# A graph convolution and a graph attention in one kernel: transposes by 32x32 blocks on VectorE and plain transfers, in place of transposing transfers

## The chip, the cores and the metric

The kernel runs on one core of a Trainium2 chip. The metric is the device time of one execution in microseconds (us), from outside; the span of the profile lies within it. TensorE is called PE in the profile (PEld is its loading of stationary operands), VectorE is DVE, ScalarE is ACT, GpSimd is POOL; SP is the queue that issues all transfers.

## What is computed

16-bit arithmetic is not used: everything is float32. x has 128 graphs of 128 nodes and 512 features; adj is one 128x128 matrix for all of them.

```
h = relu(layernorm(x));  x = x + norm_adj @ (h @ W0) + b0         # layer 0
h = relu(layernorm(x))                                            # layer 1, 8 heads of 64
q, k, v = h @ Wq + bq, h @ Wk + bk, h @ Wv + bv
scores = q k^T / 8 + (1 - adj) * -1e9                             # per graph and head
x = x + (softmax(scores) @ v) @ Wo + bo
```

norm_adj is adj scaled by the inverse roots of its row sums on both sides.

## The kernel before, in words

**Groups and blocks.** The 128 graphs are worked in 32 groups of 4. In step t of the outer loop five blocks of matmuls follow one another: W (the projection by W0 for group t+1), Q and K (queries and keys of group t), V (values of group t), Y (the projection by Wo for group t-1). Each block is a product of 512x512 by 512x512, done as a Strassen product with seven products of 256x256, four of which are divided once more into seven (class `Projection`, lines 395 on). A block has seven steps, 0 to 6. The last phases of a block's seventh product are put off: `tail` (L393, filled and emptied in `step`, L523 on) runs them in steps 1 and 2 of the next block. At the beginning of step V0 stand the attention's own matmuls: `attend` (L901) for the group before and `scores` (L831).

**Halves.** Every matmul of 128 output rows is given as two of 64 (`halves`, L136 to L140), each into its own half of the array and of the output's partitions. A float32 matmul of the code is two passes in the trace, so it stands there as two records.

**Operands.** h and the attention's output are needed with the features on the partitions. Three tiles, `op_mix`, `op_norm` and `op_att`, hold such an operand: 40 slots of 128x128, of which 28 are the seven blocks of the outer product and 12 more the inner sums (`combine`, L376 on; `combine_one`, L86 to L94, runs on GpSimd as a rule). In V the operand h is stationary and the weights move; in Q and K the weights are stationary and h moves.

**The transposes before.** h of groups 2 to 30 is transposed by transfers: `split_h` (L753 on) copies on ScalarE the two 16-bit halves of each float32 word into two planes, `write_h` (L760) writes them to DRAM, and `turn_h` (L766) reads them back with a transposing transfer. The same is done for the softmax's output: `split_att` (L875, L876) and `turn_att` (L879), into the buffer of the graph before, so that five buffers `att_buf` go round for four graphs. The first groups and the last use TensorE: `transpose_h` (L742) with 16 transposes of 16-bit halves per graph, `transpose_att` (L886) with 8 transposes of float32.

**The order.** The scheduler doesn't choose it. `plan` is a table of places: `at(t, "Q2b", f, ...)` puts a function at the second gap of step 2 of block Q in turn t (letter of block, step, and gap: none is ahead of the step's matmuls, b after them, c after the step's other reads). Each engine executes its instructions in that order, so a place decides where in every queue a step's instructions stand. VectorE reads the matmuls' results from the eight PSUM banks (`add`, L448; `read`, L463), and a bank is filled again only after its reads. Weights are reloaded from DRAM in every turn in five parts (`reload_w`, L1088).

Of the kernel before, what the change touches and what calls it, by code (L numbers as in the profile page):

```python
# [85 lines left out]
def combine_one(engine, t, left, pair, step):  # L86


    def twice(n):
        x, y = (slot_of(left, k, n) for k in pair)  # L90
        return t[:, x : y + 1 : y - x, :]

    out, x, y, minus = step
    engine.tensor_tensor(twice(out), twice(x), twice(y), ALU.subtract if minus else ALU.add)  # L94
# [3 lines left out]
def kernel(  # L98
# [38 lines left out]
    def halves(out, lhsT, rhs, **flags):  # L137

        for y in range(0, P, P // 2):
            nc.tensor.matmul(out[y : y + P // 2], lhsT[:, y : y + P // 2], rhs, **flags)  # L140
# [16 lines left out]
    planes_dram = [dp.tile([P, 2, H * P], U16, tag=f"planes_{b}", name=f"planes_{b}") for b in range(GB)]  # L157
    h_dram = [dp.tile([P, 2, H * P], U16, tag=f"planes_h_{y}", name=f"planes_h_{y}") for y in range(2)]
# [25 lines left out]
    class Weight:  # L184
# [6 lines left out]
        def slot(self, k, n):  # L191
            return self.t[:, slot_of(False, k, n), :]

# [96 lines left out]
    def combine_inner(name, engine, steps=range(9)):  # L290
        for k in steps:
            pair, step = INNER[k]
            combine_one(engine, w_sb[name].t, False, pair, step)
# [68 lines left out]
    class Operands:  # L362
        def __init__(self, name):
            self.t = op.tile([P, SLOTS, P], F32, tag=name, name=name)

        def blocks(self, i):
            return self.t[:, LEFT_AT[i] : LEFT_AT[i] + 4, :].rearrange("p (c j) n -> p c j n", c=2)

        def slot(self, i, n):
            return self.t[:, slot_of(True, i, n), :]  # L370

        def blocks_of(self, b):
# [3 lines left out]
            return self.t[:, first + j : first + 8 : 2, :]  # L376

        def combine(self, engine, inner=True, then=None, within=None):
# [6 lines left out]
            if inner:  # L385
                for step in FIRST_LEFT:
                    combine_one(within, self.t, True, (S1, S4), step)
                for step in WINOGRAD_LEFT:
                    combine_one(within, self.t, True, (A12, A22), step)


    op_mix, op_norm, op_att = (Operands(f"op_{k}") for k in "aho")
    tail = []  # L393

    class Projection:
# [13 lines left out]
        def product(self, out, product, fresh):  # L409
# [3 lines left out]
            left, right = self.left.blocks(i), self.right.blocks(k)  # L413
            for c in range(2):
                for r in range(2):
                    start = fresh and c == 0 and r == 0
                    if self.stay:
                        self.matmul(out[:, r], left[:, c], right[:, c, r * P : (r + 1) * P], start)
                    else:
                        self.matmul(out[:, r], left[:, c, r, :], right[:, c, :], start)  # L420
# [237 lines left out]
    def gcn_mix(g, b):  # L658
# [7 lines left out]
        src = pa.rearrange("p (c n) -> p c n", c=NC)  # L666
        if g == 1 and b < 2:
            nc.vector.tensor_copy(op_a[g].blocks_of(b), src)
        else:
            nc.scalar.copy(op_a[g].blocks_of(b), src)  # L670
# [60 lines left out]
    def transpose_h(g, b):  # L731
# [5 lines left out]
        planes = pt.bitcast(BF16).rearrange("p (z c n) -> p z c n", z=2, c=NC)  # L737
        words = h2.bitcast(BF16).rearrange("n (c f z) -> n z c f", c=NC, z=2)
        for z in range(2):
            for c in range(NC):  # L740
                for y in range(0, P, P // 2):
                    nc.tensor.transpose(planes[y : y + P // 2, z, c, :], words[:, z, c, y : y + P // 2], ident16)  # L742
        nc.scalar.copy(
            op_h[g].blocks_of(b).bitcast(U16).rearrange("p c (n z) -> p c n z", z=2),
            pt.bitcast(U16).rearrange("p (z c n) -> p c n z", z=2, c=NC),
        )

    def h_planes(g, half):

        t = qs[g - 1][:, 2 * half : 2 * half + 2, :].bitcast(U16)  # L750
        return t.rearrange("n c f -> n (c f)")

    def split_h(g, b):  # L753
        half, j = divmod(b, 2)
        h2 = hs.pop((g, b)).bitcast(U16).rearrange("n (c f z) -> n z c f", c=NC, z=2)
        planes = h_planes(g, half).rearrange("n (z c j f) -> n z c j f", z=2, c=NC, j=2)
        nc.scalar.copy(planes[:, :, :, j, :], h2)

    def write_h(g, half):
        nc.sync.dma_start(h_dram[half], h_planes(g, half).rearrange("n (z f) -> n z f", z=2))  # L760

    def turn_h(g, half):
        op_h[g] = op_norm
        first = LEFT_AT[S1 if half else A11]
        blocks = op_norm.t.bitcast(U16)[:, first : first + 8, :]
        nc.sync.dma_start_transpose(out=blocks, in_=h_dram[half].rearrange("n z f -> (n z) f"))  # L766

    def attention_operands(g):
        op_h[g].combine(nc.vector if g < 2 else nc.gpsimd, g > 0, within=nc.gpsimd)
# [42 lines left out]
    def att_of(g, b):  # L812


        return att_buf[(b - g) % (GB + 1)]
# [46 lines left out]
    def softmax_end(g, b):  # L862
# [3 lines left out]
        if g == 1 or g == 0 and b >= 2:  # L866
            for h in range(H):
                nc.scalar.activation(att[:, h, :], att[:, h, :], AF.Identity, bias=0.0, scale=rsm[:, h : h + 1])
        else:
            nc.gpsimd.tensor_tensor(att, att, rsm.unsqueeze(2).to_broadcast([P, H, P]), ALU.mult)  # L870

    def split_att(g, b):
        halves = att_of(g, b).bitcast(U16).rearrange("q h (k z) -> q z (h k)", z=2)
        planes = att_of(g, b - 1).bitcast(U16).rearrange("q h k -> q (h k)").rearrange("q (z j) -> q z j", z=2)
        nc.scalar.copy(planes, halves)  # L875
        nc.sync.dma_start(planes_dram[b], planes)  # L876

    def turn_att(g, b):
        nc.sync.dma_start_transpose(out=att_of(g, b - 1).bitcast(U16), in_=planes_dram[b].rearrange("q z j -> (q z) j"))  # L879
# [10 lines left out]
    def attend(g, b):  # L890
        if g not in op_o:
            op_o[g] = op_norm if g == NG - 1 else op_att
        aT = att_of(g, b if turned_in_place(g, b) else b - 1)
# [4 lines left out]
        for c in range(NC):  # L898
            for p in range(2):
                h = 2 * c + p  # L900
# [361 lines left out]
```

## Time and profile before

| | |
|---|---|
| time, median of 3 runs | 2200.97 us (2200.22 to 2202.0) |
| the profiled execution | 2200.75 us, its span 2199.0 us |
| granted TensorE clock | 0.999 |
| busy ScalarE, of the span | 1393.8 us, 63% |
| transfers | 595.48 MB, 90.6% of the 16 engines' time in the main queue; 389073 of 530613 packets under 512 bytes |
| one group | 67.4 us (1013.1 to 1080.5) |
| ScalarE's splitting copies of attention (L875) | 121, 1894 ns each, 229.2 us |
| transposing transfers | 121 of attention, 58 of h; median 5.9 and 6.8 us from issue to landing |

How to read it: in a row of a group the last number before the bar is how often it stood there, behind the bar come the busy time as a union and the mean duration of one. Matmuls overlap, so their busy time is much shorter than count times mean; the spacing of their starts is what counts. In the timeline each row has the start in us from the span's start, the length of a run of equal instructions, the engine, the line, what is written and read, and how many. A form like 128*64 tells that a matmul uses 128 rows and 64 columns of the array. In the table of stretches the columns are the stretch, its length, and busy us with the number of instructions for PE, PEld, DVE, ACT and POOL, then the granted clock, the DMA share and GB/s.

### The profile page before, as it was taken

What the parts mean: (1) busy time and instruction counts of PE and PEld (TensorE: products, weight loads), DVE (VectorE), ACT (ScalarE), POOL (GpSimd) and SP (SyncE); (2) the same over time, 40 slices, a digit from 0 to 9 for tenths busy, and PEclk for the clock granted to TensorE, in tenths of its full rate; (3) what the DMA queues carried; (4) which work ended last, traced back from release to release, by engine and by line L of the source; (5) the groups of instructions that cost most, each with busy time, mean ns of one, the idle gap of its engine ahead of it and who ended that gap; (6) DMA issues with size and microseconds to landing.
All of it is one profiled execution on the core that took longest, in us unless ns stands there. A gap on an engine that the chain in (4) does not pass through costs nothing.

```text
span 2199.0 us, 77713 instructions
## 1 busy us (share of the span) xinstructions
PE 2186.2 (99%) x31749; PEld 1879.6 (85%) x31749; DVE 1774.9 (81%) x4244; ACT 1393.8 (63%) x3604; POOL 1886.1 (86%) x2049
## 2 busy tenths in 40 slices
PE   9999999999999999999999999999999999999999
PEld 7788888888888888888888888888888888888887
DVE  7777888878888778888788887788877888878876
ACT  4577665765666666666656676566666565765654
POOL 7988988898889898888988898888889888998754
PEclk9999999999999999999999999999999999999999
DMA  5489999999999999999999999999999999999982
GB/s 165 173 260 289 290 293 292 256 284 307 263 288 287 259 297 280 293 296 244 294 312 262 294 271 269 302 286 276 290 259 289 293 279 298 263 276 298 263 261 84
DMA packets 530613, 595.48 MB, mean 271 GB/s; under 512 B 389073, under 2 KB 396369, under 8 KB 529745
## 3 DMA queue, kind: packets, MB, share of 16 engines
q1 hardware_dynamic: 530256, 590.50, 90.6%
q8 instruction: 251, 4.11, 0.8%
q14 instruction: 106, 0.86, 0.1%
HBM read 358.68 MB, written 137.89 MB: 226 GB/s over the span
## 4 chain that ended last, share of the span: by engine, by line
PE 97%; DVE 1%; issue 0%; POOL 0%; DMA 0%; ACT 0%; SPq 0%; POOLq 0%; DVEq 0%; ACTq 0%
PE bank_a L140 37%; PE bank_d L140 22%; PE bank_b L140 11%; PE bank_c L140 11%; PE pa L140 5%; PE bank_d L831 3%; PE po L901 3%; PE pss L831 1%; PE bank_b L901 1%; PE bank_a L901 1%; PE bank_b L831 1%; PE paT L886 0%; DMA xt<-in_x_dram 0%; DVE xt L448 0%; POOL w L282 0%
## 5 line engine op out<-in xcount | busy, mean ns | idle before, releaser
L858 ACT ACTIVATE att<-att,nmx 128x128 f32<-128x128 f32 x1024 | 396.1, 393 | 0.5 <-DVE nmx L850 0.5
L140 PE MATMUL bank_a<-op_h,w 128*64 128x256 f32 x2976 | 353.5, 380 | 0.0
L870 POOL TENSOR_TENSOR att<-att,rsm 128x1024 f32<-128x1024 f32 x122 | 231.7, 1900 | 110.8 <-DVE rsm L865 98.3
L875 ACT COPY att<-att 128x2048 uint16<-128x2048 uint16 x121 | 229.2, 1894 | 114.6 <-POOL att L870 114.5
L448 DVE TENSOR_TENSOR xt<-xt,bank_d 128x512 f32<-128x512 f32 x610 | 270.3, 468 | 11.0 <-PE bank_d L140 0.5
L140 PEld LDWEIGHTS bank_a<-op_h,w 128*64 128x64 f32 x2976 | 207.9, 137 | 81.6 <-issue 0.5
L140 PE MATMUL bank_d<-op_h,w 128*64 128x128 f32 (+1 forms) x3424 | 221.7, 275 | 0.1
L94 POOL TENSOR_TENSOR op_o<-op_o 128x256 f32<-128x256 f32 x297 | 212.4, 739 | 10.1
L788 ACT ACTIVATE q<-bank_a,bqk 128x256 f32<-128x256 f32 x192 | 79.8, 466 | 211.5 <-PE bank_a L140 211.3
L94 POOL TENSOR_TENSOR op_a<-op_a 128x256 f32<-128x256 f32 x279 | 198.5, 734 | 9.6
L94 POOL TENSOR_TENSOR op_h<-op_h 128x256 f32<-128x256 f32 x270 | 191.2, 733 | 11.5 <-DVE op_h L384 2.1
L140 PEld LDWEIGHTS bank_d<-op_h,w 128*64 128x64 f32 x3424 | 195.0, 137 | 7.1 <-POOL w L282 0.5
L858 ACT ACTIVATION_READ_ACCUMULATOR att<-att,nmx 128x1 f32 x1024 | 196.6, 192 | 0.0
L140 PE MATMUL bank_a<-w,op_o 128*64 128x256 f32 x1536 | 182.2, 379 | 0.0
L140 PE MATMUL bank_a<-w,op_h 128*64 128x256 f32 x1488 | 178.0, 381 | 0.0
L140 PE MATMUL bank_a<-w,op_a 128*64 128x256 f32 x1488 | 176.5, 379 | 0.0
L463 DVE TENSOR_TENSOR xt<-bank_a,xt 128x512 f32<-128x512 f32 x252 | 166.8, 683 | 3.1 <-PE bank_a L140 3.1
L850 DVE TENSOR_REDUCE nmx<-att 128x8 f32<-128x1024 f32 x128 | 154.9, 1210 | 0.0
L356 POOL TENSOR_TENSOR xt<-xt,b_o 128x1024 f32<-128x1024 f32 x62 | 147.2, 2376 | 0.0
L140 PEld LDWEIGHTS bank_a<-w,op_o 128*64 128x64 f32 x1536 | 107.5, 137 | 41.2
L351 ACT ACTIVATE h<-op_o,nb,rs 128x512 f32<-128x512 f32 x112 | 91.8, 820 | 76.2 <-POOL nb L340 76.2
L140 PEld LDWEIGHTS bank_a<-w,op_h 128*64 128x64 f32 x1488 | 102.4, 137 | 43.7
(188 smaller groups left out, 5779.8 us busy)
## 6 DMA issues: line engine op xcount, KB each, us to landing
w<-wd_v SPq DMA_DIRECT2D x155, 512.0 KB, 4.9
w<-wd_o SPq DMA_DIRECT2D x155, 512.0 KB, 9.0
w<-wd_q SPq DMA_DIRECT2D x150, 512.0 KB, 8.3
w<-wd SPq DMA_DIRECT2D x145, 512.0 KB, 5.3
planes<-att SPq DMA_DIRECT2D x121, 512.0 KB, 6.3
out_dram<-xt SPq DMA_DIRECT2D x62, 512.0 KB, 7.4
planes_h<-q SPq DMA_DIRECT2D x58, 512.0 KB, 3.2
op_o<-in_x_dram SPq DMA_DIRECT2D x56, 512.0 KB, 9.8
```

The lines of the kernel that those rows point to most:

```text
L94: engine.tensor_tensor(twice(out), twice(x), twice(y), ALU.subtract if minus else ALU.add)
L140: nc.tensor.matmul(out[y : y + P // 2], lhsT[:, y : y + P // 2], rhs, **flags)
L351: nc.scalar.activation(h, src[:, j, :], AF.Relu, bias=nb[:, j : j + 1], scale=rs[:, j : j + 1])
L356: engine.tensor_tensor(t, src, bias.unsqueeze(1).to_broadcast([P, t.shape[1], D]), ALU.add)
L448: nc.vector.tensor_tensor(dst, dst, src, f)
L463: nc.vector.tensor_tensor(t, src.rearrange("p (r f) -> p r f", r=2), t, ALU.add)
L831: nc.tensor.matmul(pss[p][:, c, :], qs[g][rows, c, cols], ks[g][rows, c, cols], start=True, stop=True)
L850: nc.vector.tensor_reduce(nmx, att_of(g, b), AX.X, ALU.max, negate=True)
L858: nc.scalar.activation(att[:, h, :], att[:, h, :], AF.Exp, bias=nmx[:, h : h + 1], scale=1.0, accum_out=sm[:, h : h + 1])
L870: nc.gpsimd.tensor_tensor(att, att, rsm.unsqueeze(2).to_broadcast([P, H, P]), ALU.mult)
L875: nc.scalar.copy(planes, halves)
L901: nc.tensor.matmul(po[p * HD : (p + 1) * HD, c * P : (c + 1) * P], vs[g][:, b, h * HD : (h + 1) * HD], aT[:, p * NC + c, :], start=True, s ...
```

## The change

The transposing transfers, the planes and their 16-bit copies go. In their place VectorE transposes 32x32 blocks into one spare buffer (`att_buf[4]`), a plain transfer writes that to DRAM, and four plain transfers read it back, each into 32 partitions, in runs of 1 KB. What arrives is transposed but stands in four quarters: the 128 columns of a slot lie in four pieces of 32, one in each quarter of the tile. `op_norm` is read and written in quarters from here on, and a stationary operand in quarters is given to TensorE as four matmuls of 32 columns in place of two of 64. That holds for V of groups 0 to 30, and for the last group's Y, whose operand is `op_norm` too. A moving operand in quarters is read with two more steps. `transpose_h` now uses float32 transposes of 128x128 (4 per graph). Weight sums of k and v and steps of attention in the first groups get other places, as do layer norm and h of all groups. In the rows with three places the first is that of turn 1, the second that of the last turn, the third that of all others.

```diff
     def halves(out, lhsT, rhs, **flags):
-        for y in range(0, P, P // 2):
-            nc.tensor.matmul(out[y : y + P // 2], lhsT[:, y : y + P // 2], rhs, **flags)
...
+        if len(lhsT.shape) == 3:
+            parts = [lhsT[:, q] for q in range(lhsT.shape[1])]
+        else:
+            parts = [lhsT[:, y : y + P // 2] for y in range(0, P, P // 2)]
+        rows = P // len(parts)
+        for y, part in enumerate(parts):
+            nc.tensor.matmul(out[y * rows : (y + 1) * rows], part, rhs, **flags)
...
+    spare = att_buf[GB].rearrange("p h k -> p (h k)")
...
-    op_mix, op_norm, op_att = (Operands(f"op_{k}") for k in "aho")
+    op_mix, op_norm, op_att = (Operands(f"op_{k}", 4 if k == "h" else 1) for k in "aho")
...
+    def flip_h(g, b):
         half, j = divmod(b, 2)
-        h2 = hs.pop((g, b)).bitcast(U16).rearrange("n (c f z) -> n z c f", c=NC, z=2)
-        planes = h_planes(g, half).rearrange("n (z c j f) -> n z c j f", z=2, c=NC, j=2)
-        nc.scalar.copy(planes[:, :, :, j, :], h2)
-
-    def write_h(g, half):
-        nc.sync.dma_start(h_dram[half], h_planes(g, half).rearrange("n (z f) -> n z f", z=2))
+        h2 = hs.pop((g, b)).rearrange("n (c i f) -> n c i f", c=NC, i=4)
+        dst = spare.rearrange("n (i c j f) -> n i c j f", i=4, c=NC, j=2)[:, :, :, j, :]
+        nc.vector.transpose(dst.rearrange("n i c f -> n c i f"), h2)
+        if j:
+            nc.sync.dma_start(h_dram[half], spare)
 
     def turn_h(g, half):
         op_h[g] = op_norm
         first = LEFT_AT[S1 if half else A11]
-        blocks = op_norm.t.bitcast(U16)[:, first : first + 8, :]
-        nc.sync.dma_start_transpose(out=blocks, in_=h_dram[half].rearrange("n z f -> (n z) f"))
+        from_dram(op_norm.slots(slice(first, first + 8)).rearrange("f q s n -> f q (s n)"), h_dram[half])
+
+    def from_dram(dst, dram):
+        for i in range(4):
+            part = dram.rearrange("(q f) x -> f q x", q=4)[:, :, i * 256 : (i + 1) * 256]
+            nc.sync.dma_start(dst[i * 32 : (i + 1) * 32], part)
 
     def attention_operands(g):
-        op_h[g].combine(nc.vector if g < 2 else nc.gpsimd, g > 0, within=nc.gpsimd)
+        op_h[g].combine(nc.vector if g < 1 else nc.gpsimd, g > 0, within=nc.gpsimd)
...
-        if g == 1 or g == 0 and b >= 2:
+        if g == 1 or g == 0 and b == 1:
             for h in range(H):
                 nc.scalar.activation(att[:, h, :], att[:, h, :], AF.Identity, bias=0.0, scale=rsm[:, h : h + 1])
         else:
-            nc.gpsimd.tensor_tensor(att, att, rsm.unsqueeze(2).to_broadcast([P, H, P]), ALU.mult)
+            engine = nc.vector if g == 0 and b >= 2 else nc.gpsimd
+            engine.tensor_tensor(att, att, rsm.unsqueeze(2).to_broadcast([P, H, P]), ALU.mult)
...
-    def split_att(g, b):
-        halves = att_of(g, b).bitcast(U16).rearrange("q h (k z) -> q z (h k)", z=2)
-        planes = att_of(g, b - 1).bitcast(U16).rearrange("q h k -> q (h k)").rearrange("q (z j) -> q z j", z=2)
-        nc.scalar.copy(planes, halves)
-        nc.sync.dma_start(planes_dram[b], planes)
+    def flip_att(g, b):
+        dst = spare.rearrange("q (i h k) -> q h i k", i=4, h=H)
+        nc.vector.transpose(dst, att_of(g, b).rearrange("q h (i k) -> q h i k", i=4))
+        nc.sync.dma_start(att_dram[b], spare)
 
     def turn_att(g, b):
-        nc.sync.dma_start_transpose(out=att_of(g, b - 1).bitcast(U16), in_=planes_dram[b].rearrange("q z j -> (q z) j"))
+        dst = att_of(g, b).rearrange("k h q -> k (h q)").rearrange("k (q x) -> k q x", q=4)
+        from_dram(dst, att_dram[b])
...
-                ("W1", "-Y6", "W5", turn_att, 0),
-                ("W4b", "-Y6b", "W1b", split_att, 1),
-                ("W5", "-Y3", "W2", exponentials, 2, 0, H // 2),
-                ("W6", "-Y4", "W3", exponentials, 2, H // 2, H),
-                ("Q2c", "-Y5b", "W4b", softmax_end, 2),
-                ("Q1", "-Y5", "W5", exponentials, 3, 0, H // 2),
-                ("Q2", "-Y6", "W6", exponentials, 3, H // 2, H),
-                ("Q0", "Q1", "Q0", turn_att, 1),
-                ("Q4b", "Q0b", "Q0b", softmax_end, 3),
-                ("Q4b", "Q0b", "Q3b", split_att, 2),
-                ("Q6b", "Q2", "Q5b", split_att, 3),
-                ("K1", "Q2", "K0", turn_att, 2),
-                ("K3", "Q5", "K2", turn_att, 3),
+                ("W4", "Q0b", "Q0b", flip_att, 0),
+                ("W6", "Q1b", "Q2", turn_att, 0),
+                ("Q3", "Q2", "Q2b", flip_att, 1),
+                ("Q5", "Q3b", "Q4", turn_att, 1),
+                ("W6", "-Y3", "W2", exponentials, 2, 0, H // 2),
+                ("Q1c", "-Y4", "W3", exponentials, 2, H // 2, H),
+                ("Q4c", "-Y5b", "W4b", softmax_end, 2),
+                ("Q6c", "-Y5", "W5", exponentials, 3, 0, H // 2),
+                ("K0c", "-Y6", "W6", exponentials, 3, H // 2, H),
+                ("K2c", "Q0b", "Q0b", softmax_end, 3),
+                ("K1", "Q4", "Q4b", flip_att, 2),
+                ("K3", "Q5b", "Q6", turn_att, 2),
+                ("K3", "Q5", "K0b", flip_att, 3),
+                ("K5", "Q5", "K2b", turn_att, 3),
...
-            at(1, "W4b", attention_operands, 1)
+            at(1, "W1b", attention_operands, 1)
...
-            at(t, "K0b" if g < NG - 1 else "Q0b", ln2, g, 0)
-            at(t, "K6b" if g < NG - 1 else "Q3b", ln2, g, 1)
+            at(t, "Q3b" if g < NG - 1 else "Q0b", ln2, g, 0)
+            at(t, "K0b" if g < NG - 1 else "Q3b", ln2, g, 1)
...
-                places = ("K6", "K6", "V0b", "V1c", "V1c", "V2", None, None, "Y5")
-                steps = ((norm_h, 0), (norm_h, 1), (norm_h, 2), (norm_h, 3), (split_h, 2), (split_h, 3))
+                places = ("K1c", "K2c", "K4c", "K5b", "K3", "K4b", "K6b", "V0b", "Y5")
+                steps = ((norm_h, 0), (norm_h, 1), (norm_h, 2), (norm_h, 3))
+                steps += tuple((flip_h, b) for b in range(GB))
                 for half in range(2):
-                    at(t, ("V1", "V2b")[half], write_h, g, half)
-                    at(t, ("V5", "Y1b")[half], turn_h, g, half)
+                    at(t, ("V6", "Y1b")[half], turn_h, g, half)
...
-        at(1, "W0", combine_inner, "v", nc.gpsimd, (6, 7, 8))
-        at(1, "W0", keep_w, "v")
+        at(0, "V6c", combine_inner, "v", nc.gpsimd, (6, 7, 8))
+        at(0, "V6c", keep_w, "v")
         at(1, "W0", load_w, "o", wo, op_att.t)
-        at(0, "V0", combine_inner, "k", nc.gpsimd)
+        at(1, "W2c", combine_inner, "k", nc.gpsimd, range(6))
+        at(1, "Q2c", combine_inner, "k", nc.gpsimd, (6, 7, 8))
```

## The prediction

> **What bounds the kernel now.** I read the page's busy shares first, then the chain that ended last, then TensorE's timeline over one group, then busy time by stage, then VectorE where the new work lands.
>
> ```profile
> span 2199.0 us, 77713 instructions
> ...
> PE 2186.2 (99%) x31749; PEld 1879.6 (85%) x31749; DVE 1774.9 (81%) x4244; ACT 1393.8 (63%) x3604; POOL 1886.1 (86%) x2049
> ...
> PE 97%; DVE 1%; issue 0%; POOL 0%; DMA 0%; ACT 0%; SPq 0%; POOLq 0%; DVEq 0%; ACTq 0%
> ```
>
> TensorE is the chain. The two transposing transfers and ScalarE's splitting copies, which the change removes, are not on it. So the question is what happens to TensorE's own time. The timeline, attention of one group and the start of V:
>
> ```profile
> 1014.88 1.04 PE L901 MATMUL bank_b<-att,v 128*64 128x128 f32 x16
> 1015.75 1.04 PE L901 MATMUL bank_a<-att,v 128*64 128x128 f32 x16
> 1016.73 1.16 PE L831 MATMUL bank_d<-k,q 64*128 64x128 f32 x16
> 1017.72 0.27 PE L831 MATMUL bank_b<-k,q 64*128 64x128 f32 x1
> 1017.73 0.27 PE L831 MATMUL bank_a<-k,q 64*128 64x128 f32 x1
> 1017.84 0.27 PE L831 MATMUL bank_b<-k,q 64*128 64x128 f32 x1
> 1017.84 0.27 PE L831 MATMUL bank_a<-k,q 64*128 64x128 f32 x1
> ...
> 1018.62 1.06 PE L831 MATMUL pss<-k,q 64*128 64x128 f32 x16
> 1019.51 1.06 PE L831 MATMUL bank_d<-k,q 64*128 64x128 f32 x16
> 1020.50 1.95 PE L140 MATMUL bank_a<-w,op_h 128*64 128x256 f32 x16
> 1022.28 1.70 PE L140 MATMUL bank_d<-w,op_h 128*64 128x128 f32 x28
> ...
> 1024.68 1.90 PE L140 MATMUL bank_a<-w,op_h 128*64 128x256 f32 x16
> 1026.41 0.28 PE L140 MATMUL bank_b<-w,op_h 128*64 128x128 f32 x2
> ```
>
> Three things are to be seen. One matmul of the code is two records (8 heads give x16): two passes. Records start in pairs: bank_b and bank_a, two different tiles of the array, within 0.01 us, the next pair 0.11 us later. And a group costs more when the tile shape (128*64, 64*128) changes. From the bank_a group at 1015.75 to bank_b at 1017.72 is 1.97 us; the two groups alone are worth 0.87 (1014.88 to 1015.75) and 0.89 (1018.62 to 1019.51), so that change of shape costs 0.21. Back into 64 columns: 1019.51 to 1022.28 is 2.77 against 0.89 + 1.73 (1024.68 to 1026.41), so 0.15.
>
> Busy time by stage (V, Y, W, Q, K; columns PE, PEld, DVE, ACT, POOL):
>
> ```profile
> 1020.50:1031.20 10.70, 10.70 (x152) 8.97 (x152) 8.48 (x17) 9.99 (x26) 10.15 (x13) 1.00 0.47 153
> 1031.20:1042.50 11.30, 11.30 (x166) 9.57 (x164) 10.61 (x26) 7.06 (x19) 7.98 (x6) 1.00 1.10 223
> 1042.50:1053.80 11.30, 11.30 (x166) 9.57 (x164) 10.63 (x25) 6.47 (x33) 10.83 (x13) 1.00 1.01 385
> 1053.80:1066.80 13.00, 13.00 (x196) 11.27 (x194) 11.06 (x31) 7.92 (x13) 10.33 (x13) 1.00 1.18 291
> 1066.80:1080.50 13.70, 13.70 (x208) 11.91 (x206) 8.56 (x26) 8.66 (x17) 13.12 (x13) 1.00 0.90 230
> ```
>
> VectorE has 1.9 us free in Q and 5.1 in K. That is where the four attention flips go (Q0b, Q2b, Q4b, K0b).
>
> **The change part by part**, against the profiled execution's 2200.75 us (0.2 below the median of 2200.97).
>
> *Quarters in V.* Where the h operand is stationary (V of groups 0 to 30, the last Y), four 32-column matmuls replace two of 64. If four tiles run as two do, the streams cost the same: 0. The Trainium skill speaks against it (TensorE: Matmul & The Clock Gate, The mechanism): matmuls stay in strict program order, only weight loads are pulled ahead. In the built program the two passes of one matmul stand one behind the other, so by that rule a quarter's second pass holds up the next quarter and never more than two run: four quarters take 4 x 0.109 where two halves took 2 x 0.109 (0.87 us / 8). The row says otherwise: in program order it is b, b, a, a; the trace has b, a, b, a. The array passed a waiting second pass by. I take 0 by the row, and the rule's sum as a rival: no row shows it passing three.
>
> Nor does a row show four pieces issued in one slot (0.027 us each). The nearest is the bf16 transposes of L742, 16 starts in 0.65 - 0.22 us, 0.029 each. So between 0 and 7% of V's N=128 part (about 6 us a group, at most 0.4); I take 0.
>
> *Changes of shape.* Rows show 0.15 us for each change into 64 columns, 0.21 into 128. The built program has 258 instead of 81: V to Y once a group, and V's last phases lie in Y1 and Y2 among 64-column matmuls, four more; the rest are the f32 transposes. The skill (TensorEngine Tiling (Array Packing), Key Properties) says that changing the tiling mode drains the array. No row shows 64 to 32: 0 if the pieces of a half need no drain, 0.21 at most. I take 0.15, since every change in the trace cost at least that: 177 x 0.148 = +26.2 us (0 to 37).
>
> *f32 transposes for bf16 halves*: 12 banks, 4 x 0.109 = 0.44 (the transposes of L886 start 0.109 apart) for 16 x 0.029 = 0.46: 0.
>
> *VectorE's flips.* 121 of 1024 elements: nearest row the 1024-wide reduction of L850, 1.21 us; 116 of 512: nearest row BN statistics, 0.69. Sum 226 us, which takes VectorE from 1775 to about 2000. What counts is the queue in Q. Flip 1 (Q2b) stands ahead of five reads of bank_d:
>
> ```profile
> 1059.39 1.47 DVE L448 TENSOR_TENSOR q<-q,bank_d 128x256 f32<-128x256 f32 x5
> ```
>
> They end at 1060.86; TensorE began refilling these banks at 1060.72 (d1, whose last read is the third of the five, at about 1060.33), so it has 0.4 us to spare. Flip 0 shifts the queue by 0.2 (1.21 less the 0.92 in which VectorE waited there for a load), flip 1 by 1.2. TensorE then stands 1.0 us: 1.4 - 0.4. And flip 1 is a new wait: all flips fill the one spare buffer, so it waits until flip 0's write to DRAM has landed. Flip 0 ends at about 1056.0; VectorE reaches flip 1 at 1059.3. Landing times of the two plain writes there were:
>
> ```profile
> planes<-att SPq DMA_DIRECT2D x121, 512.0 KB, 6.3
> planes_h<-q SPq DMA_DIRECT2D x58, 512.0 KB, 3.2
> ```
>
> So the wait is 0 to 3.0; the middle, 4.75, gives 1.4 us, with the bank reads queued behind it. ln2 moved from K0b to Q3b adds 1.7 us (two statistics, two aggregates) to Q, where only 1.9 - 2.4 was left; flip 2 then stands before bank_b's last read. There VectorE's spare time in K catches up; I take 0. Together 1.0 + 1.4 = 2.4 us a group, less about 0.1 that the drains give back: 2.3 x 29 groups = +67 us (0.9 to 4 each: 26 to 116).
>
> *Off TensorE's path.* ScalarE loses L875's 229 us and the h copies (63% busy, nobody waits for it). GpSimd's combinations of h get rows of 32 elements; its last one ended at 1052.85, first use 1055.50, a cover of 2.65 us over 6.6 us of such work. A slowdown under 40% costs nothing. DMA: 256-byte packets become 1 KB ones; the chain has 0% DMA. A turn is four issues instead of one, at about 0.5 us each on SP; those queued behind are reloads with several us to spare.
>
> *The first groups.* At 98 to 103 us four operand sums of h stood on VectorE (4.6 us) ahead of TensorE's bank read: 3.0 us lost, then a dip of the granted clock (about 1.7), and 1.8 at 116.4 before pa. They go to GpSimd, and the exponentials later: -6.5 us (0 to -8). Moved with them: k's nine sums on GpSimd (9 x 0.73 = 6.6 us) from V0 of group 0 to W2 and Q2 of group 1, first read in K1, over 15 us later; v's last three sums and its 2560 KB store (landing 8.9 us) forward to V6, past nothing on SP but loads of later groups; the normalisations of attention 2 and 3 from ScalarE to VectorE, 1024 elements each, some 1.2 to 2 us, in Q4 and K2 of group 1's turn, where h's flips do not stand yet in full. I take 0 for each, and 2 us in all where the cover fails. Next late is what bounds the other groups.
>
> Sum: 2200.75 + 26.2 + 67 - 6.5 = 2287 us.
>
> **The rivals.**
>
> *It is faster.* Place: V's last phases in Y1 and Y2. If quarters need no drain beside halves, and the spare buffer's writes land within 3.3 us so that VectorE's flips fit into its idle time, only the first groups' stalls remain: 2200.75 - 6.5 + 22 transposing changes x 0.15 = 2197.5, 2194 with 8 saved. It decides below about 0.03 us a change together with no stall in Q. For it: five of seven us of idle VectorE in Q and K. Against: all 81 changes in the trace cost; five reads with 0.4 us of slack.
>
> *Quarters run two at a time* (the strict order). V has 24 slots of 0.216 (1.73 / 8) and 56 of 0.109 in a group, 11.3 us; doubled, 30 x 11.3 + 2 x 12.1 (the undivided V of group 0 and the last Y, 56 slots of 0.216) = +363: 2564, or 2650 with the stalls in Q. For it: the skill's rule, the program's order. Against: the pair rows.
>
> *VectorE absorbs all, the changes stay*: 2220. *The whole round trip is late*: flip 3, write, turn must land before attention; each leg 3 to 6 us, 1 to 2 us a group more: 2320 to 2380.
>
> **How the numbers follow.** Main case, 2242 to 2352 (the ends of the two sums): 0.48. Changes alone, 2205 to 2242: 0.13. Round trip late, to 2400: 0.06. Faster rival 0.11, and 0.04 between -0.2% and +0.2%, about what a measurement of this kernel can tell from no change. Two at a time: 0.16; another cause above 2400: 0.02. Range 2190 to 2400, which leaves out 0.18. Faster 0.11, same 0.04, slower 0.85.
>
> **What would show it.** Right: four records of 128*32 starting together, the next four 0.11 (N=128) or 0.22 us later; 0.15 us lost at each 32/64 border in Y; flips of about 1.2 and 0.65 us; waits of the 1024-element flip for a DMA of `turned`, and after it TensorE waiting in Q1 to Q4 for L480 reads of bank_d. Wrong: 32-column records in pairs (the doubled V), no loss at the borders, or TensorE still at 99% with no waits in Q.

## The result, and the profile after

The changed kernel takes 2548.31 us (median of 4 runs, 2542.56 to 2554.15) against 2200.86 us on the same chip: 1.158 times as long (95% interval 1.155 to 1.161). The forecast was 2287 us, with a range of 2190 to 2400. The profiled execution took 2554.15 us, its span is 2552.3 us. Of the page of the changed kernel, the lines that answer to those shown of the kernel before:

```profile
span 2552.3 us, 88489 instructions
...
PE 2329.6 (91%) x36629; PEld 1909.0 (75%) x36629; DVE 1974.9 (77%) x4479; ACT 1085.1 (43%) x3359; POOL 1886.6 (74%) x2052
...
q1 hardware_dynamic: 261040, 590.53, 68.5%
...
PE 55%; DVE 20%; DMA 19%; issue 2%; POOL 2%; SPq 1%; ACT 1%; DVEq 0%; POOLq 0%; ACTq 0%
```

TensorE's share of the chain falls from 97% to 55%. VectorE and transfers take 39% of it, though VectorE is busy for 77% of the span and the transfers' main queue fills 68.5% of its engines' time. So waits have come in. Four rows of the same page name them (behind the bar: busy time, mean ns, idle time ahead of the group and what ended it; the last row is a transfer, with its size and the median time to landing):

```profile
L774 DVE STREAM_TRANSPOSE att<-h 128x512 f32<-128x512 f32 x116 | 81.8, 705 | 211.2 <-DMA turned_h<-att 207.7
L852 PE MATMUL bank_d<-k,q 64*128 64x128 f32 x1024 | 117.1, 356 | 120.2 <-DVE att L859 120.1
...
L897 DVE STREAM_TRANSPOSE att<-att 128x1024 f32<-128x1024 f32 x121 | 150.1, 1240 | 63.9 <-DMA turned<-att 58.6
...
turned_h<-att SPq DMA_DIRECT2D x58, 512.0 KB, 6.5
```

VectorE's flips of h stand 208 us for the write of the spare buffer to land, and TensorE's scores stand 120 us for VectorE. (The median of 6.5 us lies between two kinds: the write of a group's first two flips lands in 9.7 us, that of the last two in 2.6, medians counted from the trace's records.) How the one wait becomes the other is seen around V0 of one group. First SyncE's transfers (start, length of the issuing, line, what, how many), then VectorE's timeline, then TensorE's:

```profile
1091.58 1.38 SPq L1112 DMA_DIRECT2D w<-wd_v  x3
1093.00 2.04 SPq L1112 DMA_DIRECT2D w<-wd_o  x2
1095.13 0.61 SPq L776 DMA_DIRECT2D turned_h<-att  x1
1095.80 2.66 SPq L1112 DMA_DIRECT2D w<-wd_o  x3
```

```profile
1091.80 0.70 DVE L774 STREAM_TRANSPOSE att<-h 128x512 f32<-128x512 f32 x1
...
1096.77 0.41 DVE L480 TENSOR_TENSOR k<-k,bank_c 128x256 f32<-128x256 f32 x1
1105.20 0.71 DVE L774 STREAM_TRANSPOSE att<-h 128x512 f32<-128x512 f32 x1 [8.02 <-DMA turned_h<-att]
1105.83 1.25 DVE L859 SCALAR_TENSOR_TENSOR att<-bank_d,msk 128x512 f32<-128x512 f32 x2
```

```profile
1100.38 1.06 PE L852 MATMUL pss<-k,q 64*128 64x128 f32 x16
1106.54 2.67 PE L852 MATMUL bank_d<-k,q 64*128 64x128 f32 x16 [5.10 <-DVE att L859]
1109.14 3.19 PE L149 MATMUL bank_a<-w,op_h 128*32 128x256 f32 x32
1112.15 1.70 PE L149 MATMUL bank_d<-w,op_h 128*32 128x128 f32 x56
```

The second flip of h ends at 1092.5. Its write is issued only at 1095.1, behind five reloads of weights, and lands at 1105.2, some 9 us later, among eight reloads of 512 KB. The third flip (place K6b) needs the same buffer and stands at the head of VectorE's queue for 8.0 us; behind it stand the reads of the scores (L859), and for these TensorE waits 5.1 us. Then it goes on at about half speed: 16 records of bank_d take 2.67 us where they took 1.06, and V's first product takes 3.19 us for 1.95. The granted clock goes with it (the column before the last two), 0.83, then 0.53, then 1.00:

```profile
1101.00:1107.00 6.00, 0.90 (x10) 0.71 (x8) 1.80 (x3) 1.08 (x2) 5.69 (x6) 0.83 0.87 356
1107.00:1112.00 5.00, 5.00 (x48) 3.21 (x51) 4.29 (x7) 0.00 (x0) 4.84 (x8) 0.53 0.12 46
1112.00:1116.00 4.00, 4.00 (x124) 3.30 (x120) 1.12 (x4) 1.17 (x2) 1.81 (x3) 1.00 0.46 137
```

Where the 353 us between the two spans lie is in this table, with some of the experiments (below) beside them. Each number is the time from the first TensorE record of a part to the first of the next, summed over all turns (us):

| | before | q_before | after | h_own | three | three_late | three_halves | after_noload |
|---|---|---|---|---|---|---|---|---|
| up to group 0's scores | 71 | 72 | 72 | 73 | 73 | 72 | 72 | 73 |
| scores | 121 | 121 | 294 | 136 | 136 | 136 | 136 | 146 |
| V | 335 | 338 | 383 | 358 | 380 | 373 | 337 | 341 |
| Y, W, start of Q | 815 | 834 | 830 | 833 | 834 | 833 | 811 | 830 |
| rest of Q, and K | 661 | 661 | 765 | 774 | 717 | 698 | 698 | 724 |
| `attend` | 108 | 108 | 111 | 110 | 155 | 176 | 162 | 109 |
| last turn's rest | 88 | 89 | 98 | 98 | 94 | 98 | 97 | 94 |

### The profile page after: what moved, and what is told of

The parts are those of the page before. It is cut to its first block, busy times and chain, and to the rows that moved or that the text cites. A ratio compares the mean times of both kernels' runs of the same rounds, so it can differ in the third digit from the quotient of the medians.

```text
span 2552.3 us, 88489 instructions
## 1 busy us (share of the span) xinstructions
PE 2329.6 (91%) x36629; PEld 1909.0 (75%) x36629; DVE 1974.9 (77%) x4479; ACT 1085.1 (43%) x3359; POOL 1886.6 (74%) x2052
## 3 DMA queue, kind: packets, MB, share of 16 engines
q1 hardware_dynamic: 261040, 590.53, 68.5%
## 4 chain that ended last, share of the span: by engine, by line
PE 55%; DVE 20%; DMA 19%; issue 2%; POOL 2%; SPq 1%; ACT 1%; DVEq 0%; POOLq 0%; ACTq 0%
PE bank_a L149 22%; PE bank_d L149 12%; DMA turned_h<-att 7%; PE bank_b L149 7%; PE bank_c L149 7%; DMA turned<-att 7%; DVE xt L480 5%; DVE att L897 4%; DMA w<-wd_o 3%; PE bank_d L852 3%; DVE st L345 3%; DVE q L480 2%; PE pa L149 2%; DVE xt L495 2%; DVE k L480 2%
## 5 line engine op out<-in xcount | busy, mean ns | idle before, releaser
L149 PE MATMUL bank_d<-op_h,w 128*64 128x128 f32 (+1 forms) x3424 | 223.2, 275 | 58.4 <-DVE q L480 58.4
L774 DVE STREAM_TRANSPOSE att<-h 128x512 f32<-128x512 f32 x116 | 81.8, 705 | 211.2 <-DMA turned_h<-att 207.7
L852 PE MATMUL bank_d<-k,q 64*128 64x128 f32 x1024 | 117.1, 356 | 120.2 <-DVE att L859 120.1
L823 ACT COPY v<-bank_a 128x512 f32<-128x512 f32 x96 | 56.3, 586 | 395.2 <-PE bank_a L149 358.2
L149 PE MATMUL bank_a<-w,op_h 128*32 128x256 f32 x2976 | 221.1, 449 | 0.0
L852 PEld LDWEIGHTS bank_d<-k,q 64*128 64x128 f32 x1024 | 99.3, 247 | 134.4 <-DVE att L859 125.9
L897 DVE STREAM_TRANSPOSE att<-att 128x1024 f32<-128x1024 f32 x121 | 150.1, 1240 | 63.9 <-DMA turned<-att 58.6
L149 PEld LDWEIGHTS bank_a<-w,op_h 128*32 128x32 f32 x2976 | 100.4, 127 | 82.8 <-issue 45.4
```

Source lines behind the costliest of these rows:

```text
L149: nc.tensor.matmul(out[y * rows : (y + 1) * rows], part, rhs, **flags)
L774: nc.vector.transpose(dst.rearrange("n i c f -> n c i f"), h2)
L823: nc.scalar.copy(dst, src)
L852: nc.tensor.matmul(pss[p][:, c, :], qs[g][rows, c, cols], ks[g][rows, c, cols], start=True, stop=True)
L897: nc.vector.transpose(dst, att_of(g, b).rearrange("q h (i k) -> q h i k", i=4))
```

## The experiments

The theory after the result: VectorE stands, at the head of its queue, for the one spare buffer's write, which lands late on loaded queues. The rivals: the quarters are dear themselves (the forecast's strict order gave 2564 us, by chance near the 2548 measured), or VectorE is simply too full. All ratios are to the kernel before, with 95% intervals.

**The quarters alone: q_before.**

```diff
-        for y in range(0, P, P // 2):
-            nc.tensor.matmul(out[y : y + P // 2], lhsT[:, y : y + P // 2], rhs, **flags)
+        for y in range(0, P, rows):
+            nc.tensor.matmul(out[y : y + rows], lhsT[:, y : y + rows], rhs, **flags)
...
+            self.rows = 32 if w in ("v", "o last") else 64
```

> The kernel before with only its stationary operand cut finer: where h is stationary (the projection V, and the last output projection) four 32-column matmuls take the place of two of 64. Transposes, VectorE and the transfers are as before. The waiting theory (VectorE waits for the spare buffer's write, the quarters themselves run four at a time): only the borders between 32 and 64 columns are added, which cost 0.6 us a group in the trace of the changed kernel (2.75, 0.57, 1.68 and 0.36 us against 2.60, 0.44, 1.53 and 0.22, and 0.05), 29 groups: 2201 + 18 = 2219 us. The rival (the quarters are dear: two run at a time): +363, 2564 us, which is close to the 2548 measured.

Measured: 2225.24 us, 1.0108 (1.0093 to 1.0124), +24.4. Groups by form of q_before:

```profile
L140 PE MATMUL bank_a<-w,op_h 128*32 128x256 f32 x2976 | 178.5, 380 | 0.0
L140 PE MATMUL bank_d<-w,op_h 128*32 128x128 f32 x3360 | 102.8, 273 | 0.0
```

Twice as many records as before take the same busy time (178.0 and 101.9 us with 1488 and 1680 records of 128*64). In the trace's single records four of 128*32 start within 0.02 us, the next four 0.11 us later. So quarters run four at a time. What they cost is the borders: q_before has 161 more changes of shape, 24.4 / 161 = 0.15 us each. The quarters' rival falls for this schedule. The 16 more changes that the changed kernel's float32 transposes bring were not measured apart.

**The h flip's buffer: h_own.**

```diff
+        buf = op_att.t[:, 32:40].rearrange("p s n -> p (s n)") if g > 2 and half == 0 else spare
...
-            nc.sync.dma_start(h_dram[half], spare)
+            nc.sync.dma_start(h_dram[half], buf)
```

> The changed kernel, but the flips of h for batches 0 and 1 of a group (from group 3 on) fill eight slots of the attention's operand tile that are free at that time, and not the spare buffer; batches 2 and 3 and the attention flips still share the spare buffer. So the flip at the end of K no longer waits for the write that was issued some 10 us before. Same work on every engine. The waiting theory: the score stage goes back from 9.4 to about 3.8 us and V's first product from half clock to full (12.3 to 10.7 us): 7.2 us in each of 28 groups, 2548 - 202 = about 2345 us, with the stalls in Q left. The rival (VectorE is simply too full: 226 us of flips): the wait only changes its name, 2520 to 2548 us. The quarters' rival: 2548.

Measured: 2373.8 us, 1.0787 (1.0761 to 1.0814). Half of the whole loss goes with one buffer for one pair of flips, with the same work on every engine: VectorE was not too full. TensorE's row for the scores, h_own, by form:

```profile
L853 PE MATMUL bank_d<-k,q 64*128 64x128 f32 x1024 | 72.8, 281 | 10.8 <-DVE att L860 10.8
```

Of 120.1 us of waits one is left, in turn 1, where spare is still shared; the mean duration is back from 356 to 281 ns, as the clock no longer dips. The gain is 28 us less than expected: V gets only to 358 us and not to 335 (see three_halves), and Q and K take 9 us more. The same run tells the two writes apart, since the first now has a name of its own:

```profile
turned_h<-att SPq DMA_DIRECT2D x30, 512.0 KB, 4.8
turned_h<-op_o SPq DMA_DIRECT2D x28, 512.0 KB, 9.6
```

**No shared buffer at all: three.** As h_own, and in `flip_att`:

```diff
+        buf = op_att.t[:, 24:32].rearrange("p s n -> p (s n)") if g > 0 and b % 2 else spare
```

> The same, and the attention flips of batches 1 and 3 fill eight more free slots of that tile, so that neighbouring flips never share a buffer. The waiting theory: beside h_own's gain Q and K lose the part of their 3.4 us a group that is the wait for the write (predicted 1.4 of 2.4, measured as 58.6 us of VectorE's waits): another 40 to 60 us, about 2295 us; left are the borders (18 us) and the shift by the flips themselves. The rival (VectorE too full): no gain over h_own.

Measured: 2389.04 us, 1.0851 (1.0833 to 1.0869): not 50 us better than h_own but 15 worse. The table shows both halves of that: Q and K fall from 774 to 717 us, as expected, but `attend` rises from 110 to 155 and V from 358 to 380. The waits of TensorE in three (us in total, times, longest):

```profile
PE po L929 <- DMA att<-turned: 28.1, 17, 4.5
PE bank_b L149 <- DVE q L480: 19.9, 29, 3.0
PE bank_d L149 <- DVE q L480: 16.0, 30, 0.8
```

bank_d's wait in Q is down from 58.4 to 16.0 us. But TensorE now reaches the attention before the last turn has landed: a wait that the other one had hidden. (In the waits of `po` that the trace puts to GpSimd, 6.9 us more here, a part of a turn landed within 0.3 us before TensorE went on, so the turns account for these too: 35 us in three, 47 in three_late.)

**Y in quarters too: three_y.** As three, and in `Projection.matmul`:

```diff
-            halves(out, lhsT, rhs, start=start, stop=True, skip_group_check=True)
+            halves(out, lhsT, rhs, 32 if self.w == "o" else 64, start=start, stop=True, skip_group_check=True)
```

> The same as three, and the output projection's stationary operand is cut in quarters too, so that V's last phases and Y have one tile shape and the five borders in Y go; one stays at Y's end. If quarters cost nothing and the borders 0.6 us a group: 15 us less than three. If quarters are dear: about 300 us more (Y has as many matmuls as V).

Measured: 2406.74 us, 1.094 (1.0903 to 1.0977): 18 us more, not 15 less. The borders don't go: Y's put-off phases lie in W's steps, and the five borders stand there now. And with 98411 instructions for 88491 the idle time of stationary loads that ended with nothing but "issue" rises from 84 to 127 us. Neither of the two answers that were expected; the second is followed up next.

**All projections in quarters: q_all.** The kernel before, in `halves`:

```diff
-        for y in range(0, P, P // 2):
-            nc.tensor.matmul(out[y : y + P // 2], lhsT[:, y : y + P // 2], rhs, **flags)
+        for y in range(0, P, 32):
+            nc.tensor.matmul(out[y : y + 32], lhsT[:, y : y + 32], rhs, **flags)
```

> The kernel before with the stationary operand of every projection (and of the adjacency product) cut into four pieces of 32 columns. No borders are left inside the projections, one stays on each side of the attention. If quarters cost nothing but borders: about 0.2 us a group, 2201 + 6 = 2207 us. If TensorE can't be fed with twice as many matmuls (in three_y, with a quarter more instructions on TensorE than three, the time went up by 18 us instead of down, and the idle time that the trace puts to issue from 84 to 127 us): 50 us more or worse.

Measured: 2514.06 us, 1.1432 (1.1409 to 1.1456). Page of q_all, the queue of TensorE's program (packets, MB, share) and the chain:

```profile
q8 instruction: 465, 7.62, 1.2%
...
PE 88%; issue 9%; DVE 1%; POOL 1%; DMA 0%; ACT 0%; SPq 0%; POOLq 0%; DVEq 0%; ACTq 0%
```

and its timeline at one such place:

```profile
565.09 0.94 PE L140 MATMUL bank_d<-w,op_a 128*32 128x128 f32 x23
567.92 0.43 PE L140 MATMUL bank_d<-w,op_a 128*32 128x128 f32 x8 [1.88 <-issue]
```

TensorE stops in the middle of a product, with nothing to wait for. The queue "q8 instruction" moves blocks of 16 KB, 251 of them in before, 465 in q_all. That goes with TensorE's records (31749 and 59125), so I take it for its program. Counted where two matmuls start over 0.41 us apart (0.11 is usual) with nothing waited for, q_all has 184 stops, 264 us beyond the usual. In 109 of them (207 us) such a block landed during the stop; the next expectation's 146 with 243 us is a looser count. More telling is the end: 182 of the 184 ended 1.2 to 1.8 us after a block had landed (median 1.4), while the landings are 5.4 us apart.

**The same without the reloads: q_all_noload.**

```diff
-        nc.sync.dma_start(w_sb[name].t[:, some, :], w_dram[name][:, some, :])
+        if n < 12:
+            nc.sync.dma_start(w_sb[name].t[:, some, :], w_dram[name][:, some, :])
```

> q_all without the reloads of the weights from the twelfth on, so from the fourth turn on all projections read what stands in the weight buffers (values are wrong from there, the work on the engines is the same, about 300 of 590 MB of transfers are gone). In q_all TensorE stood still 267 us in 187 places for nothing that the profile shows; in 146 of them (243 us) a 16 KB block of its own program landed in that time, and it went on some 1.4 us later. If those blocks come late because the transfers' queues are full: most of the 313 us go, 2220 to 2260 us. If TensorE simply can't issue that many matmuls: 2514 as before.

Measured: 2316.32 us, 1.053 (1.051 to 1.055). With the same instructions 198 of the 313 us go, so most of it is program blocks landing late on loaded queues. More is left than I expected: by the same count 71 stops with 89 us, with the transposing transfers still there. Of these 67 end in the same way, 1.2 to 1.8 us after a block. (The kernel before was not run without its reloads, here and in the next run; with TensorE busy 99% it has little to gain.)

**The changed kernel without the reloads: after_noload** (the same edit).

> The changed kernel, with the same reloads left out (same note on the values). It has one spare buffer and the order of flips as changed. If the flip's 8 us wait is a late landing of the write (issued 3 us late behind eight reload issues on SyncE, then 6.5 us in the queues with them), the write lands about 3 us after its flip, VectorE is free before the scores, and the stall at V0 goes (7.2 us a group), and part of the 1.9 us of waits in Q: 2548 - 210 to -260 = 2290 to 2340 us. If one spare buffer is too few whatever the load: at most 60 us go, 2490.

Measured: 2319.59 us, 1.0535 (1.0521 to 1.055), as the waiting theory had it. Groups and transfers of after_noload:

```profile
L774 DVE STREAM_TRANSPOSE att<-h 128x512 f32<-128x512 f32 x116 | 81.7, 704 | 32.3 <-DMA turned_h<-att 29.8 <-DMA turned<-att 2.5
```

```profile
turned_h<-att SPq DMA_DIRECT2D x58, 512.0 KB, 2.8
```

The write of the first two flips, which the third waits for, lands in 3.1 us for 9.7 (2.8 for 6.5 over both kinds), the flips' wait falls from 208 to 30 us (three waits, in the turns that still reload), and the scores (146 us) and V (341) come back nearly to where they were. So one spare buffer does for h's flips where its write lands in 3 us.

**Flips behind the bank reads: three_late.**

```diff
-                ("Q3", "Q2", "Q2b", flip_att, 1),
+                ("Q3", "Q2", "Q2c", flip_att, 1),
...
-                ("K1", "Q4", "Q4b", flip_att, 2),
+                ("K1", "Q4", "Q4c", flip_att, 2),
```

> three, with two attention flips put behind the bank reads of their step instead of ahead of them: flip 1 behind the five reads of bank_d in Q2, flip 2 behind the reads of Q4. (In three and three_y one attention flip of the last turn overwrote a slot that the output projection still read, which changes values of the last groups and no work; here the last turn keeps to the spare buffer.) The shift theory (in three, Q and K take 23.63 us in every group against 21.95, since flips stand ahead of reads that TensorE waits for): Q and K back to about 22.3, and the flips' round trip 0.5 us later before the attention, in all 20 to 35 us less than three's 2389. Rival (VectorE is full, the order doesn't matter): as three.

Measured: 2387.41 us, 1.0831 (1.0804 to 1.0859): as three. Q and K do fall from 717 to 698 us, as the shift theory has it, and `attend` takes them back (155 to 176).

**An earlier last turn: turn_early.**

```diff
-                ("K3", "Q5", "K0b", flip_att, 3),
-                ("K5", "Q5", "K2b", turn_att, 3),
+                ("K3", "Q5", "Q6b", flip_att, 3),
+                ("K5", "Q5", "K1", turn_att, 3),
```

> three_late with flip 3 and its turn one place earlier (Q6b and K1). In three, three_late and three_halves TensorE waits 0.5 to 2 us a group at the attention for the last turn to land. If the round trip's start decides: attention back from about 4.8 to 3.7 us, 25 to 30 us less than three_late's 2387, unless flip 3 now delays reads in K. If the landing is set by the queues' load in K and not by the start: as three_late.

Measured: 2378.32 us, 1.0807 (1.0792 to 1.0822), 9 us less than three_late and not 25 to 30; the single runs of the two overlap (2375.64 to 2382.49 against 2371.84 to 2388.39). This experiment does not test what it was meant to. In the traces VectorE, ScalarE, GpSimd and SyncE execute the same instructions in the same order as in three_late, since none of them has anything to do between the old places and the new ones; flip 3 ends 17.8 us after Q's start (median) in both. So the 9 us are what two measurements of one order differ by. What holds the last turn is seen in three_late, around one attention (VectorE's flip 3, SyncE's transfers, TensorE):

```profile
1088.21 1.23 DVE L899 STREAM_TRANSPOSE op_o<-att 128x1024 f32<-128x1024 f32 x1
...
1091.28 1.73 SPq L788 DMA_DIRECT2D att<-turned  x4
1093.11 0.38 SPq L900 DMA_DIRECT2D turned<-op_o  x1
1096.70 3.52 SPq L788 DMA_DIRECT2D att<-turned  x4
...
1103.20 1.97 PE L929 MATMUL po<-att,v 128*64 128x128 f32 x16 [2.73 <-POOL op_a L94]
```

Flip 3 is done at 1089.4, but its write is issued only at 1093.1. Ahead of it in SyncE's queue stand the four reads of turn 2, and these stand until flip 2's write has landed. Turn 3 then waits for flip 3's write, and its last quarter lands at 1102.95, just before TensorE goes on. So the four round trips of a group run one after another, some 6 us each. How long the row of them takes depends on the queues' load: counted from Q's start the last quarter lands at 30.7 us in three_late, 30.2 in turn_early, 29.6 in the changed kernel and 27.4 in the same kernel without reloads, after_noload (medians), where `attend` waits for nothing (109 us) though Q and K are nearly as short as in three (724 us for 717). An order of SyncE's queue that lets a later write pass was not tried.

**Half the pieces in V: three_halves.**

```diff
-            parts = [lhsT[:, q] for q in range(lhsT.shape[1])]
+            parts = [lhsT[:, q] for q in (0, 2)]
...
+            return self.cut[:, :, s - s % 2 : s - s % 2 + 2, :].rearrange("p q s n -> p q (s n)")
```

> three_late, with V's stationary operand read as two pieces of 64 neighbouring columns instead of four of 32; the pieces hold columns of two blocks, so V's sums are mixed and the values of v are not those of the reference; the count of matmuls in V halves and the borders in Y are gone, all else is the same. If V's waits in h_own and three (10.8 us in the undisturbed kernel, 11.4 to 14.4 there) come from feeding TensorE twice as many instructions while the transfers are busy: 0.72 us of borders and 1 to 1.5 us of waits a group, 50 to 65 us less than three_late. If they come from late weights or operands: only the borders, 21 us less.

Measured: 2323.68 us, 1.0555 (1.0531 to 1.0579), 64 us less than three_late: the borders (22 us in the row of Y) and 36 us in V. Three V blocks, of three, q_before and three_halves (PE and PEld with their counts, then DVE, ACT, POOL, granted clock, DMA share, GB/s):

```profile
968.03:982.41 14.38, 11.81 (x298) 9.95 (x296) 9.73 (x20) 8.51 (x36) 12.78 (x14) 0.94 0.88 292
```

```profile
962.41:973.18 10.77, 10.77 (x298) 8.51 (x296) 8.54 (x17) 10.00 (x26) 10.22 (x13) 1.00 0.61 212
```

```profile
937.99:948.68 10.69, 10.69 (x151) 8.96 (x151) 9.06 (x18) 5.14 (x20) 9.10 (x12) 1.00 0.98 343
```

298 records with the transfers 61% busy: no stop. 151 records at 98%: no stop. 298 at 88%: 3.6 us more. The last is the longest V block of three (median 12.2 us), and the share alone does not decide: in h_own some V blocks at 86 to 89% took 10.78 us. What the stops have in common is how they end. By the count used for q_all, three has 29 stops in V (35 us); in 12, with 21 us, a program block landed, and 28 of the 29 ended 1.2 to 1.7 us after such a landing. With half the records (three_halves) there is no such stop, and with all of them and the reloads gone (after_noload) each of 26 V blocks takes 10.78 us. Quarters are free only where TensorE's program arrives in time.

**The first groups' moves alone: first_moves, first_moves2.** The kernel before with those lines of the diff, carried over to its splits and turns (some of them below); first_moves2 takes the last edit back.

```diff
-        op_h[g].combine(nc.vector if g < 2 else nc.gpsimd, g > 0, within=nc.gpsimd)
+        op_h[g].combine(nc.vector if g < 1 else nc.gpsimd, g > 0, within=nc.gpsimd)
...
-            at(1, "W4b", attention_operands, 1)
+            at(1, "W1b", attention_operands, 1)
...
-        at(0, "V0", combine_inner, "k", nc.gpsimd)
+        at(1, "W2c", combine_inner, "k", nc.gpsimd, range(6))
+        at(1, "Q2c", combine_inner, "k", nc.gpsimd, (6, 7, 8))
```

> The kernel before, with only the moves of the first groups: sums of k, v and h, the exponentials, normalisations, splits and turns of groups 0 and 1 at the places that the changed kernel gives them; transposes, transfers and tile shapes as before. Prediction on record: -6.5 us (0 to -8), 2194.5. The traces of the changed kernel and of h_own show the gain between the scores of groups 1 and 2 as about 4 us (V's last part and Y of that turn 16.12 to 12.33 us, W 3.19 to 2.60, but 0.4 us more at the end of W), and group 0's scores 1.2 us later, so 3 to 4 us net: 2197. A rival: the moved exponentials press on group 1's attention and nothing is gained, 2201.

> first_moves with one move taken back: k's nine sums stand at V0 of group 0 again, as in the kernel before. In first_moves the turn of group 1 became 2.6 us shorter, but in the next turn's scores TensorE stood 6.9 us longer: ScalarE's copy into the attention's operand tile waited 5.6 us for that tile's 2560 KB store of the output weight, which was issued at 132.95 us, behind sums that k's had pushed back on GpSimd. If that is the cause, the 6.9 us go and 2.6 us stay: 2198 us, the only version here that would beat both. If the store is late for another reason: 2205 as first_moves.

Measured: 2204.9 us, 1.0018 (1.0010 to 1.0026), so 4 us slower, and 2201.59 us, 1.0003 (0.9995 to 1.0011), no difference. Taking k's sums back does remove the long stop at the next scores (10.69 to 3.77 us), so its cause holds, but in turn 1 the first two stretches of Q, up to the put-off phases of W, then take 4.30 and 3.52 us (first_moves 2.60 and 1.99, before 3.19 and 1.53), and in both runs the rest of Q and K of that turn takes 2 us more (28.4 and 28.5 for 26.3), which together eat the gain. (The expectation misnames two parts: the 16.12 and 12.33 us are W of turn 1, the 3.19 and 2.60 us the first stretch of Q.) The moves gain nothing either way, and no version here beats the kernel before.

## Why the prediction was wrong

**Quarters at no cost: right.** They run four at a time, as the pair rows said and against the rule of the Trainium skill that the forecast weighed (TensorE: Matmul & The Clock Gate, The mechanism), by which matmuls keep strict order: q_before measures 0.1 us a V, not 363 in all. What neither the rows nor the rule said is the feeding of TensorE. The changed kernel's own trace has no stop of over 0.3 us without a named cause, but in h_own and three, with the stop at V0 gone, they come, and take back part of the repair.

**Changes of shape, +26.2: right.** 0.151 us each in q_before (0.148 forecast).

**Flips of 1.21 and 0.69 us: right.** 1.240 and 0.705.

**The Q stall, 2.4 us a group: the right mechanism, somewhat small.** Q and K cost 103 us more, against 67. Three splits it over 29 groups: (765 - 717) / 29 = 1.6 us is the wait for the buffer (1.4 forecast; 2.0 with h_own's 774 as the base), (717 - 661) / 29 = 1.9 us the shift (1.0 forecast). Of the shift 0.7 us are the two flips ahead of reads (three_late); the other 1.3 stay with both behind, so they are other work in those queues, perhaps layer norm, which I didn't try apart.

**The step that failed: "What counts is the queue in Q."** The forecast wrote that all flips fill one buffer and that a flip therefore waits for the write before it, and then priced that wait for flip 1 in Q alone. The four flips of h in K and V0 fill the same buffer, and one of them stands ahead of the scores' reads. Their wait has no term in the sum and no reason for its absence. The nearest the forecast came to one is "There VectorE's spare time in K catches up; I take 0", said of flip 2 and layer norm; it would not have helped, for spare time of an engine is of no use where the head of its queue is waiting. The missing term measures 174.5 us (2548.3 - 2373.8 in h_own): 5.6 us a group at the scores and 0.9 in V, stop and low clock together. Its size comes from the landing. For flip 1 the forecast took the middle of 3.2 and 6.3 us; here the write stood 1.7 us (median; 2.6 in the group shown) behind other transfers in SyncE's queue and then took 9.7. The forecast's "reloads with several us to spare" looked at the reloads alone; what was queued behind them had no time to spare.

**First groups, -6.5: not gained, +4 us alone (first_moves).** The stop at 98 us does go (W of turn 1, 16.12 to 12.33 us), but k's moved sums push wo's sums and their 2560 KB store later. In first_moves that costs 6.9 us at the next scores. In the changed kernel the same turn has the longest wait of all, 15.3 us of a flip for its write, and the scores 18.1 us long; that the store stands ahead of that write too is likely, not tried.

**The round trip, held off as a rival: not late as the kernel stands** (`attend` 111 us for 108; the last quarter lands 0.4 us before it, by the medians), but it is what comes next: with the other waits gone it costs 1.6 to 2.3 us a group (three, three_late), against the 1 to 2 named. The forecast named three legs of the trip; that the trips of a group queue behind one another on SyncE it left out.

**The ends of the main case.** 2242 to 2352 are called the ends of the two sums; these give 2219 (0, 26 and -8) to 2354 (37, 116 and 0). The measured time lies far outside both.

## What to carry to other kernels

A shared staging buffer puts the landing of a transfer into the queue of the engine that fills it: for every filling, not only the first, ask who wrote it last, when that write is issued on its queue, what is queued with it, and what stands behind the waiting instruction. Take the landing from transfers with the same neighbours, not from the median of all. If a read-back waits on the same queue for its write to land, ask what else stands behind it there. Check that moving a place changes some queue's order. When a first wait is removed, read what it hid (here the last turn, and TensorE's own program) before counting the gain.

## What was not expected of the hardware

- TensorE's program, as I read the instruction queue, comes in 16 KB blocks through the same 16 transfer engines. With twice as many matmuls per us and the queues loaded, TensorE stopped 184 times in q_all, 264 us in all, and 182 times went on 1.2 to 1.8 us after a block had landed.
- After 5.1 us without work the granted clock was 0.53 in the stretch from 0.5 to 5.5 us after the restart: the stop at the scores cost 5.1 us, and the matmuls behind it another 2.85 (2.67 + 3.19 - 1.06 - 1.95).
- A plain write of 512 KB landed in 2.6 us when it was issued after the reloads, and in 9.7 in their midst, in one and the same kernel (medians, changed kernel); the median of both, 6.5, describes neither.
